# Turning x and the product with V in VectorE's blocks of 32 instead of on TensorE, in an attention kernel on one Trainium2 core

## The chip, the cores and the metric

The kernel runs on one core of a Trainium2 chip. Its time is the device time of one execution in microseconds (us). The median of three runs of the kernel before is 764.2 us (762.27 to 765.88). The profile is of one further execution, which took 762.58 us; the profile's span, from the first instruction of the program to the last, is 760.8 us of that.

Names: PE is TensorE, DVE is VectorE, ACT is ScalarE, POOL is GpSimd, SP is the engine whose queue issues most of the DMA transfers. PSUM is PE's output memory, eight banks of 128 x 512 f32.

## What is computed

x is 8 x 512 x 512 (batch, rows, model), cond is 8 x 512. There are 16 heads of 32 columns.

```
Q  = heads(x @ Wq.T + bq);     K  = heads(x @ Wk.T + bk);     V = heads(x @ Wv.T + bv)
tQ = heads(cond @ Wq.T + bq);  tK = heads(cond @ Wk.T + bk)      # one row per batch entry
scores = einsum('bhqd,bhkd->bhqk', Q + tQ, K + tK) / sqrt(32)
out = x + merge_heads(softmax(scores) @ V)
```

## The kernel before

The work is cut into T = 32 tiles: tile t is batch entry b = t // 4 and a group g = t % 4 of four heads (128 columns). PE, ACT, DVE and POOL run in the order that is written by hand (`manual_schedule`); SP's DMA queue runs in the order in which the program names the transfers.

**A tile.** Scores are made twice. `row_max` makes the scores of a chunk of 128 query rows (4 matmuls, one per head, into four banks), and DVE takes the negated maximum of each row (`row_max_of`, two reductions over two banks each). `denominators` has ACT take the exponential of the same banks with that maximum as bias; only the row sums (`sums`) are kept. `split_max` (POOL) splits the maximum into bf16 parts, and `transpose_max` turns them, so that `exponentials` can make the scores again in transposed form, keys by queries, with the maximum added by a matmul, and ACT writes their exponential to SBUF (`es`). `times_v` multiplies `es` by V: four heads go to four groups of 32 PSUM partitions, so the result is 128 (head, column) x 512 (query).

**The way out.** `weighted` does the four `times_v` of a tile and copies the result out of PSUM (`leave`, L556). Later `output` turns it back to query rows with four PE transposes (`untranspose`, L566), `divide` multiplies by the reciprocal of the sums (`invert`, L576; `divide`, L580), and `finish` (L591) adds x + bv on POOL and stores. x + bv is `xr`, loaded and summed by `load_residual` (L131, L135).

**The way in.** x comes in chunks of 128 rows (`load_x`, L123: 128 partitions, runs of 2 KB). `transpose_x` turns a chunk with four PE transposes (L251) and ACT or DVE copies it out of PSUM (L254) to `xT`. `combine_x` forms sums of quarters of `xT` for the projections, which multiply 2 x 2 blocks with seven products instead of eight (`first_products`, `other_products`, L335 and L338).

**The loop.** An iteration t has four stages, one for each key chunk of tile t; every stage has `exponentials(t, kc)`, a `row_max(t + 1, ...)`, the four `denominators` of it, and some other work between: stage 0 projects a part of the next batch entry's q and turns a chunk of x, stage 1 does `weighted(t - 1)`, stage 2 projects a part of k, stage 3 a part of v and `transpose_max`. `output(t - 1)` lies in stage 2 (t odd) or stage 3 (t even). Four iterations make one batch entry. The first tile and the weights are set up in an opening; the last three tiles have an order of their own after the loop.

**The banks.** `TURNS` lists, for eight consecutive stages (two iterations), which banks a stage uses: entries 0 to 3 for its exponentials (and then, as each comes free, for the stage's other work), entries 4 to 7 for the row scores. Pairs of entries that are read together are neighbouring banks before.

**The opening.** It loads x, cond and the weights, turns the weights (`transpose_w`, L206), projects tiles 0 and 1 in full (`project_qk`, L281) and makes the conditioning terms.

Of the kernel before, what the change touches and what calls it, by code (L numbers as in the profile page):

```python
# [17 lines left out]
def kernel(  # L18
# [32 lines left out]

    nc = tc.nc
# [25 lines left out]
    TURNS = [  # L78
        (7, 2, 0, 1, 3, 4, 5, 6),
        (7, 0, 3, 4, 5, 6, 1, 2),  # L80
        (3, 0, 4, 5, 1, 2, 6, 7),
        (2, 5, 0, 1, 6, 7, 3, 4),
        (7, 0, 5, 6, 3, 4, 1, 2),
        (3, 0, 4, 5, 1, 2, 6, 7),
        (4, 5, 0, 1, 6, 7, 2, 3),
        (5, 0, 6, 7, 1, 2, 3, 4),

        (2, 5, 6, 7, 3, 4, 0, 1),
        (2, 5, 3, 4, 0, 1, 6, 7),
        (2, 5, 0, 1, 6, 7, 3, 4),  # L90
        (2, 5, 6, 7, 3, 4, 0, 1),
        (2, 5, 3, 4, 6, 7, 0, 1),

        (2, 5, 0, 1, 6, 7, 3, 4),
        (2, 5, 3, 4, 6, 7, 0, 1),
        (0, 1, 5, 2, 6, 7, 3, 4),
        (0, 1, 5, 2, 6, 7, 3, 4),
        (5, 0, 6, 7, 1, 2, 3, 4),
# [3 lines left out]
    def banks(i, n=1):  # L102

        j = TURNS[turn[0]][i]
        return psum[:, j, :] if n == 1 else psum[:, j : j + n, :]
# [18 lines left out]

    xr = {}

    def load_residual(t):

        b, g = divmod(t, G)
        xr[t] = op.tile([P, NS, P], F32, tag="xr", name=f"xr_{t}", bufs=3)  # L130
        nc.sync.dma_start(  # L131
            xr[t], x[b].rearrange("(c p) d -> p c d", p=P)[:, :, g * P : (g + 1) * P]
        )
        bias = bvb[:, g * P : (g + 1) * P].unsqueeze(1).broadcast_to([P, NS, P])
        nc.gpsimd.tensor_tensor(xr[t], xr[t], bias, ALU.add)  # L135
# [28 lines left out]
    nc.sync.dma_start(cond_sb[:B, :], cond)  # L164
    nc.sync.dma_start(cond_sb[B : B + 1, :], bq.rearrange("(o d) -> o d", o=1))
    nc.sync.dma_start(cond_sb[B + 1 : B + 2, :], bk.rearrange("(o d) -> o d", o=1))
    load_w("q", Wq, nc.sync, [0])
    load_w("k", Wk, nc.scalar, [0])
    load_w("q", Wq, nc.scalar, [1])
    load_w("q", Wq, nc.sync, [2, 3])  # L170
# [3 lines left out]
    nc.sync.dma_start(bvb, bv.rearrange("(o d) -> o d", o=1).broadcast_to([P, D]))  # L174

# [8 lines left out]
    for i in range(2):  # L184
        m = const.tile([P, NS, HG, HD], BF16, tag=f"split{i}", name=f"split{i}")
        nc.vector.memset(m, 0.0)
        split.append(m)
    condT = const.tile([P, NC, HD], F32, tag="condT", name="condT")
# [54 lines left out]
    def transpose_x(n, pt, leaves=nc.vector.tensor_copy):  # L243

        b, sc = divmod(n, NS)
        if b >= B:
            return
        if sc == 0:
            xT[b] = xtp.tile([P, NC, S], F32, tag="xT", name=f"xT_{b}")
        for cc in range(NC):  # L250
            nc.tensor.transpose(  # L251
                pt[:, cc * P : (cc + 1) * P], xs[n][:, cc * P : (cc + 1) * P], ident
            )
        leaves(xT[b][:, :, sc * P : (sc + 1) * P], pt.rearrange("p (c s) -> p c s", c=NC))  # L254
        load_x(n + NS)
# [107 lines left out]
    def first_products(n, b, u, dens, small, at, first=0):  # L363

        one_, two_ = banks(first), banks(at)
        c1, c12, c2, c22 = parts_of(n, b, u)
        m1 = c2[:, 0, :]
        product(n, b, u, 1, one_[:, :HS])  # L370
        nc.scalar.copy(m1, one_[:, :HS])
        dens()
        small()
        product(n, b, u, 6, two_[:, :HS])
        w = P if n == "k" else HS
        product(n, b, u, 2, two_[:, HS : HS + w], (0,), slice(0, w))
        product(n, b, u, 7, one_[:, HS:])
        nc.vector.tensor_tensor(c12, two_[:, :HS], m1, ALU.add)
        nc.vector.tensor_tensor(c1[:, 0, :w], two_[:, HS : HS + w], m1[:, :w], ALU.add)
        if w < HS:  # L380
            nc.gpsimd.tensor_copy(c1[:, 0, w:], m1[:, w:])
        plus(n, b, u, 1, c22, one_[:, HS:], c12)
# [175 lines left out]
    def weighted(t, pt):  # L558

        for kc in range(NS):  # L560
            times_v(t, kc, pt)
        leave(t, pt)
# [68 lines left out]
    for c in range(NS):  # L631
        transpose_x(c, bank(1 + c), nc.scalar.copy if c % 2 else nc.vector.tensor_copy)
    pc = bank(6)
# [12 lines left out]
    transpose_w("q", 0, bank(7), 1)  # L646
    transpose_w("k", 0, bank(1), 0)
    transpose_w("q", 1, bank(2), 1)
    pq, pk = bank(5), bank(0)
    for cc in range(NC):  # L650
        project_qk_part(0, "q", cc, pq)
    transpose_w("q", 2, bank(3), 0)
    transpose_w("q", 3, bank(4), 1)
    for cc in range(NC):
        project_qk_part(0, "k", cc, pk)
    transpose_w("k", 1, bank(6), 0)
    condition("q", bank(7))
    transpose_w("k", 2, bank(1), 1)
    transpose_w("k", 3, bank(2), 0)
    transpose_w("v", 0, bank(3), 1)  # L660
    condition_end("q", bank(4), nc.vector)
    project_qk_end(0, "q", pq)
    condition("k", bank(6))
    transpose_w("v", 1, bank(7), 1)
    condition_end("k", bank(3), nc.gpsimd)
    transpose_w("v", 2, bank(1), 0)
    project_qk_end(0, "k", pk)
    transpose_w("v", 3, bank(4), 1)
    transpose_x(NS, bank(2), nc.scalar.copy)
# [9 lines left out]
    transpose_x(NS + 1, banks(0), nc.scalar.copy)  # L679
    denominators(0, 0)  # L680
    project_qk(1, "q", banks(3))
# [3 lines left out]
    transpose_x(NS + 2, banks(2), nc.scalar.copy)  # L685
# [8 lines left out]
    first_products("v", 0, 0, lambda: denominators(0, 3), nothing, 2, 0)  # L694
    advance()
    row_max(1, 0)
    transpose_max(0, banks(3), nc.scalar.copy)
    other_products("v", 0, 0, lambda: denominators(1, 0), nothing, (2, 0))
# [28 lines left out]
    for t in range(T - 3):  # L727
# [6 lines left out]
        if r % 2:  # L734
            turn_x = lambda: transpose_x(t + NS + 3, banks(1), nc.vector.tensor_copy)
            project_pair("q", *qk_of, dens, turn_x, 3)
        else:
            transpose_x(t + NS + 3, banks(0), nc.scalar.copy)
            if t:
                project_pair("q", *qk_of, dens, nothing, (1, 3))  # L740
            else:
                other_products("k", 0, 1, dens, nothing, (1, 3))
# [5 lines left out]
        if t:  # L748
            dens()
            invert(t - 1, sums[t - 1])  # L750
            weighted(t - 1, banks(0))
# [10 lines left out]
        if r % 2:  # L762
            project_pair("k", *qk_of, dens, lambda: output(t - 1, banks(1)), 3)
        elif t:
            project_pair("k", *qk_of, dens, nothing, (0, 2))
        else:
            other_products("v", 0, 1, dens, nothing, (0, 2))
# [5 lines left out]
        if t == T - 4:  # L773
            transpose_max(t + 1, banks(0), nc.scalar.copy)
            denominators(t + 2, 0)
            output(t - 1, banks(1))
# [4 lines left out]
        def small():  # L781
            transpose_max(t + 1, banks(1))
            if t and r % 2 == 0:
                output(t - 1, banks(2))

        project_pair("v", b + 1, r, dens, small, (0, 2) if r % 2 else 3)
# [47 lines left out]
    exponentials(t, 1, (3, 4, 6, 7))  # L834
# [4 lines left out]
    exponentials(t, 2, (3, 4, 0, 1))  # L839
    times_v(t, 1, pv)  # L840
    transpose_max(t + 1, pd)
    exponentials(t, 3, (6, 7, 3, 4))
    times_v(t, 2, pv)
    exponentials(t + 1, 0, (0, 1, 6, 7))
# [4 lines left out]
    exponentials(t, 1, (3, 4, 0, 1))  # L849
# [7 lines left out]
    exponentials(t, 2, (6, 7, 3, 4))  # L857
# [4 lines left out]
    exponentials(t, 3, (0, 1, 6, 7))  # L862
# [11 lines left out]
    pi, po = psum[:, 3, :], [psum[:, 4, :], psum[:, 6, :]]  # L874
# [55 lines left out]
```

## Time and profile before

| | |
|---|---|
| median of three runs | 764.2 us (762.27 to 765.88) |
| profiled execution: time, span | 762.58 us, 760.8 us |
| PE busy | 750.4 us, 99% of the span |
| ACT busy | 630.2 us, 83% |
| DVE busy | 525.2 us, 69% |
| POOL busy | 132.9 us, 17% |
| PE transposes of x: L251 | 128 in 32 groups of four |
| PE transposes of the product with V: L566 | 124 in 31 groups of four |
| DMA packets | 40376, of 29.51 MB |

Rows of the profile have the line in the kernel, the engine, the operation, output <- inputs and the shape; a group's busy time counts overlapped instructions once, and the end of a matmul is modelled. In the timeline the first two columns are the start and the length in us. "[0.67 <-PE psum L515]" at the end of a row means that the engine stood idle for 0.67 us before it, and that the instruction named ended that.

### The profile page before, as it was taken

The numbers are of one execution on the slowest core, as the hardware profiler recorded it, in microseconds if no ns is written. First come the engines' busy times: TensorE is split into PE (matmuls) and PEld (weight loads), VectorE is DVE, ScalarE is ACT, GpSimd is POOL, SyncE is SP. The second block draws the span as 40 slices with busy tenths as digits, with TensorE's granted clock in tenths as the row PEclk, the third lists the DMA queues.
The fourth block names the chain that finished last, engine by engine and source line by source line (L and its number), as shares of the span: only waits on it lengthen the run. The fifth ranks groups of instructions, "written<-read, shape, count | busy, mean of one in ns | idle before, by whom it ended". The sixth has DMA issues, their size and how long they took to land.

```text
span 760.8 us, 14393 instructions
## 1 busy us (share of the span) xinstructions
PE 750.4 (99%) x5494; PEld 435.9 (57%) x5494; DVE 525.2 (69%) x730; ACT 630.2 (83%) x1462; POOL 132.9 (17%) x229
## 2 busy tenths in 40 slices
PE   8999999999999999999999999999999999999997
PEld 5566556655556665565665555665555665555432
DVE  2577767677667777676776776777766777757764
ACT  2559888888889888888888888888888988888965
POOL 2711011111101111101111111111110111110220
PEclk9999999999999999999999999999999999999999
DMA  9200011102011110111111011110101111000110
GB/s 310 64 2 15 15 43 43 43 15 56 15 42 43 43 31 13 47 39 43 42 32 40 15 43 42 43 44 14 43 1 28 29 28 28 1 29 29 29 42 28
DMA packets 40376, 29.51 MB, mean 39 GB/s; under 512 B 1770, under 2 KB 34538, under 8 KB 40308
## 3 DMA queue, kind: packets, MB, share of 16 engines
q1 hardware_dynamic: 39460, 27.42, 12.6%
q10 hardware_dynamic: 848, 1.18, 0.5%
q8 instruction: 43, 0.70, 0.4%
q14 instruction: 25, 0.20, 0.1%
HBM read 20.21 MB, written 8.39 MB: 38 GB/s over the span
## 4 chain that ended last, share of the span: by engine, by line
PE 96%; ACT 1%; DMA 1%; DVE 0%; issue 0%; DVEq 0%
PE psum L338 25%; PE psum L534 15%; PE psum L515 15%; PE psum L433 14%; PE psum L335 14%; PE psum L512 6%; PE psum L566 2%; PE psum L251 2%; PE psum L281 2%; PE psum L496 1%; ACT e L527 1%; DMA w_k<-in_L_cond_Wk_dram 1%; PE psum L206 1%; ACT e L529 0%; DMA x<-in_x_dram 0%
## 5 line engine op out<-in xcount | busy, mean ns | idle before, releaser
L442 DVE TENSOR_REDUCE nmax<-psum 128x2 f32<-128x1024 f32 x256 | 301.7, 1219 | 160.1 <-PE psum L433 159.4
L470 ACT ACTIVATE dead<-psum,nmax 128x512 f32<-128x512 f32 x496 | 335.0, 692 | 12.9 <-DVE nmax L442 12.8
L527 ACT ACTIVATE e<-psum 128x512 f32<-128x512 f32 x270 | 145.8, 595 | 81.5 <-PE psum L515 81.5
L433 PE MATMUL psum<-kT,qT 32*128 32x512 f32 x1024 | 138.1, 595 | 0.7 <-ACT kT L296 0.4
L515 PE MATMUL psum<-qT,kT 32*128 32x512 f32 x1024 | 132.5, 588 | 0.0
L529 ACT ACTIVATE e<-psum 128x1024 f32<-128x1024 f32 x121 | 124.7, 1030 | 0.0
L534 PE MATMUL psum<-e,v 128*32 128x512 f32 x1024 | 118.6, 596 | 0.4 <-ACT e L529 0.3
L470 ACT ACTIVATION_READ_ACCUMULATOR dead<-psum,nmax 128x1 f32 x496 | 103.6, 209 | 0.0
L484 POOL CAST split<-nmax 128x16 bf16<-128x16 f32 x32 | 8.2, 255 | 510.8 <-DVE nmax L442 510.8
L433 PEld LDWEIGHTS psum<-kT,qT 32*128 32x128 f32 x1024 | 63.8, 183 | 51.8 <-issue 29.4
L534 PEld LDWEIGHTS psum<-e,v 128*32 128x32 f32 x1024 | 29.5, 109 | 82.1 <-issue 57.9
L512 PE MATMUL psum<-maxT,onesb 3*128 3x512 bf16 x512 | 51.4, 384 | 1.6 <-DVE res L580 0.8
L515 PEld LDWEIGHTS psum<-qT,kT 32*128 32x128 f32 x1024 | 51.1, 185 | 2.5 <-issue 0.2
L591 POOL TENSOR_TENSOR res<-res,xr 128x512 f32<-128x512 f32 x30 | 38.1, 1271 | 66.1 <-DVE res L580 66.1
L335 PE MATMUL psum<-wc_v,xc 128*128 128x256 f32 x192 | 49.4, 380 | 0.0
L512 PEld LDWEIGHTS <-onesb 3*128 3x128 bf16 x512 | 13.4, 91 | 60.5 <-issue 50.9
L338 PE MATMUL psum<-xc,wc_q 128*128 128x256 f32 x180 | 46.4, 380 | 0.3 <-ACT e L529 0.3
L338 PE MATMUL psum<-xc,wc_k 128*128 128x256 f32 x180 | 46.3, 379 | 0.0
L556 DVE COPY oT<-psum 128x512 f32<-128x512 f32 x29 | 20.1, 691 | 35.6 <-PE psum L534 35.6
L135 POOL TENSOR_TENSOR xr<-xr,bvb 128x512 f32<-128x512 f32 x32 | 40.6, 1270 | 0.0
L335 PE MATMUL psum<-wT_v,xT 128*128 128x256 f32 x128 | 37.9, 398 | 0.0
L335 PEld LDWEIGHTS psum<-wc_v,xc 128*128 128x128 f32 x192 | 35.4, 190 | 4.3
(147 smaller groups left out, 831.0 us busy)
## 6 DMA issues: line engine op xcount, KB each, us to landing
xr<-in_x_dram SPq DMA_DIRECT2D x32, 256.0 KB, 3.1
out_dram<-res SPq DMA_DIRECT2D x31, 256.0 KB, 2.4
x<-in_x_dram SPq DMA_DIRECT2D x30, 256.0 KB, 2.7
w_v<-in_L_cond_Wv_dram SPq DMA_DIRECT2D x4, 256.0 KB, 5.5
w_q<-in_L_cond_Wq_dram SPq DMA_DIRECT2D x3, 256.0 KB, 4.4
w_k<-in_L_cond_Wk_dram SPq DMA_DIRECT2D x3, 256.0 KB
x<-in_x_dram ACTq DMA_DIRECT2D x2, 256.0 KB, 4.1
w_k<-in_L_cond_Wk_dram ACTq DMA_DIRECT2D x1, 256.0 KB, 4.5
```

Source lines behind the costliest of these rows:

```text
L135: nc.gpsimd.tensor_tensor(xr[t], xr[t], bias, ALU.add)
L335: nc.tensor.matmul(pt, xb, w, start=(kc == kcs[0]), stop=(kc == kcs[-1]))
L338: nc.tensor.matmul(pt, w, xb, start=(kc == kcs[0]), stop=(kc == kcs[-1]))
L433: nc.tensor.matmul(pt, qkT["q", t][r, qc * P : (qc + 1) * P], qkT["k", t][r, :], start=True, stop=True,)
L442: nc.vector.tensor_reduce(nmax[t][:, qc, pr * 2 : pr * 2 + 2, 0], pt, AX.X, ALU.max, negate=True)
L470: nc.scalar.activation(dead, banks(HG + j), AF.Exp, bias=nmax[t][:, qc, j, :], accum_out=sums[t][:, qc, j, :],)
L512: nc.tensor.matmul(bank[j], onesb[r, :], maxT[t][r, :], start=True, stop=False)
L515: nc.tensor.matmul(bank[j], qkT["k", t][r, kc * P : (kc + 1) * P], qkT["q", t][r, :], start=False, stop=True,)
L527: nc.scalar.activation(e[:, i, :], bank[pr * 2 + i], AF.Exp)
L529: nc.scalar.activation(e, banks(2, 2), AF.Exp)
L534: nc.tensor.matmul(pt[j * HD : (j + 1) * HD, :], vs[b % 2][:, kc, (g * HG + j) * HD : (g * HG + j + 1) * HD], es[t, kc, j // 2][:, j % 2, ...
L591: last.tensor_tensor(y, y, xr.pop(t), ALU.add)
```

## The change

Four things change.

1. **x is loaded by blocks and turned by DVE** (from batch entry 1 on). `spread` views a 512 x 512 matrix so that partition j of a group of 32 holds the rows j, 32 + j, 64 + j and so on, 32 columns of each: a run of 128 bytes per row. `load_block` loads the 128 columns of a chunk so, with four DMAs of 32 partitions. One DVE transpose of 32 x 32 blocks (`turn_x`) then gives a chunk of `xT` in SBUF; neither PE nor PSUM is used. The chunks are now columns, not rows.
2. **The product with V is turned by DVE** for the tiles 0 to 27 (`weighted`). The transpose reads PSUM and writes `y` with queries modulo 32 on partitions. The sums have to take the same arrangement: POOL spreads them (`apart`, 128 x 64), and four small matmuls (128 x 32 weights `modulo`, 16 columns, one per head), placed after the first `times_v`, bring them to a bank `pd`; DVE takes the reciprocal from there. POOL then multiplies, adds `xr` (now loaded by blocks too) and four DMAs store runs of 128 bytes. `leave`, `untranspose`, `divide` and `output` fall away for these tiles; tiles 28 to 31 keep the old way.
3. **TURNS** is another table, since the turns of x and of the product need no bank of their own; pairs may lie apart, and are read with a step. The entries used by the projections change with it.
4. **The opening** issues cond, bq and bk from ACT's queue, the first chunk of Wk and the second of Wq from SP's, adds constants (`which`, `modulo`, `bvs`), and projects q of tile 1 at the place where a chunk of x was turned.

```diff
+    def spread(a, d):
+        return a.rearrange("(f j) d -> j f d", j=BL)[:, :, d : d + BL]
+
+    def load_block(n):
+        b, cc = divmod(n, NC)
+        if b < B:
+            xs[n] = xp.tile([P, NB, BL], F32, tag="x", name=f"x_{n}")
+            for h in range(HG):
+                nc.sync.dma_start(xs[n][h * BL : (h + 1) * BL], spread(x[b], cc * P + h * BL))
...
+    def turned_by_vector(t):
+        return t < T - 4
...
+        if turned_by_vector(t):
+            xr[t] = op.tile([P, NB, BL], F32, tag="xr", name=f"xr_{t}", bufs=3)
+            for h in range(HG):
+                nc.sync.dma_start(
+                    xr[t][h * BL : (h + 1) * BL], spread(x[b], g * P + h * BL)
+                )
...
-    nc.sync.dma_start(cond_sb[:B, :], cond)
-    nc.sync.dma_start(cond_sb[B : B + 1, :], bq.rearrange("(o d) -> o d", o=1))
-    nc.sync.dma_start(cond_sb[B + 1 : B + 2, :], bk.rearrange("(o d) -> o d", o=1))
+    nc.scalar.dma_start(cond_sb[:B, :], cond)
+    nc.scalar.dma_start(cond_sb[B : B + 1, :], bq.rearrange("(o d) -> o d", o=1))
+    nc.scalar.dma_start(cond_sb[B + 1 : B + 2, :], bk.rearrange("(o d) -> o d", o=1))
     load_w("q", Wq, nc.sync, [0])
-    load_w("k", Wk, nc.scalar, [0])
-    load_w("q", Wq, nc.scalar, [1])
-    load_w("q", Wq, nc.sync, [2, 3])
+    load_w("k", Wk, nc.sync, [0])
+    load_w("q", Wq, nc.sync, [1, 2, 3])
...
-        load_x(n + NS)
+        load_block(n + NC)
+
+    def turn_x(n):
+        b, cc = divmod(n, NC)
+        if b >= B:
+            return
+        if cc == 0:
+            xT[b] = xtp.tile([P, NC, S], F32, tag="xT", name=f"xT_{b}")
+        nc.vector.transpose(xT[b][:, cc, :], xs[n].rearrange("p f i -> p (f i)"))
+        load_block(n + NC)
...
-    def weighted(t, pt):
+    def weighted(t, pt, pd):
+        apart = op.tile([P, HG, NS, NS], F32, tag="apart", name=f"apart_{t}")
+        nc.gpsimd.tensor_tensor(
+            apart,
+            sums[t].rearrange("p c h o -> p h c o").broadcast_to([P, HG, NS, NS]),
+            which.unsqueeze(1).unsqueeze(1).broadcast_to([P, HG, NS, NS]),
+            ALU.mult,
+        )
         for kc in range(NS):
             times_v(t, kc, pt)
-        leave(t, pt)
+            if kc == 0:
+                for h in range(HG):
+                    nc.tensor.matmul(
+                        pd[h * BL : (h + 1) * BL, : NB],
+                        modulo,
+                        apart[:, h].rearrange("p c a -> p (c a)"),
+                        start=True,
+                        stop=True,
+                    )
+        rec = op.tile([P, NB, 1], F32, tag="recs", name=f"recs_{t}")
+        nc.vector.reciprocal(rec, pd[:, :NB].unsqueeze(2))
+        y = op.tile([P, NB, BL], F32, tag="res", name=f"res_{t}")
+        nc.vector.transpose(y.rearrange("p f e -> p (f e)"), pt)
+        nc.gpsimd.tensor_tensor(y, y, rec.broadcast_to([P, NB, BL]), ALU.mult)
+        nc.gpsimd.tensor_tensor(y, y, xr.pop(t), ALU.add)
+        b, g = divmod(t, G)
+        for h in range(HG):
+            nc.sync.dma_start(spread(out[b], g * P + h * BL), y[h * BL : (h + 1) * BL])
...
-            invert(t - 1, sums[t - 1])
-            weighted(t - 1, banks(0))
+            weighted(t - 1, banks(0), banks(1))
...
-            project_pair("k", *qk_of, dens, lambda: output(t - 1, banks(1)), 3)
-        elif t:
-            project_pair("k", *qk_of, dens, nothing, (0, 2))
-        else:
-            other_products("v", 0, 1, dens, nothing, (0, 2))
+        if t:
+            project_pair("k", *qk_of, dens, nothing, 1 if r % 2 else (0, 3))
+        else:
+            other_products("v", 0, 1, dens, nothing, (0, 3))
```

The rows of TURNS that the prediction speaks of, for the stages 1 and 2 of an even and of an odd iteration:

```diff
-        (7, 0, 3, 4, 5, 6, 1, 2),
-        (3, 0, 4, 5, 1, 2, 6, 7),
+        (7, 2, 0, 1, 3, 4, 5, 6),
+        (3, 0, 1, 2, 6, 7, 4, 5),
...
-        (3, 0, 4, 5, 1, 2, 6, 7),
-        (4, 5, 0, 1, 6, 7, 2, 3),
+        (6, 7, 0, 1, 4, 5, 2, 3),
+        (4, 7, 0, 1, 2, 3, 5, 6),
```

## The prediction, made before the change was run

> **What bounds the kernel now.** I read the busy table first, then the busy time by stretches of one batch entry, then the timeline of two iterations, then the groups and the DMA queues.
>
> ```profile
> span 760.8 us, 14393 instructions
> ...
> PE 750.4 (99%) x5494; PEld 435.9 (57%) x5494; DVE 525.2 (69%) x730; ACT 630.2 (83%) x1462; POOL 132.9 (17%) x229
> ```
>
> ```profile
> core 0: us, PE busy (x) PEld busy (x) DVE busy (x) ACT busy (x) POOL busy (x), PEclk, DMA share, GB/s
> 175.00:265.00 90.00, 90.00 (x676) 53.23 (x672) 64.78 (x90) 78.87 (x184) 14.25 (x26) 1.00 0.13 36
> ```
>
> One stretch of 90 us is nearly one batch entry (four tiles; it repeats every 90.4 us in the timeline). PE has no gap in it; ACT has 11.1 us, DVE 25.2 us, and the granted clock is 1.00. So time goes where PE's time goes, but only what PE really issues less counts, and busy time overstates that, since ends of matmuls are modelled and overlap. The timeline gives the true price, from one start to the next:
>
> ```profile
> 306.80 0.60 PE L251 MATMUL psum<-ident,x 128*128 128x128 f32 x4
> 307.24 1.03 PE L338 MATMUL psum<-xc,wc_q 128*128 128x256 f32 x4
> ...
> 315.11 0.39 PE L512 MATMUL psum<-maxT,onesb 3*128 3x512 bf16 x4
> 315.31 0.69 DVE L556 COPY oT<-psum 128x512 f32<-128x512 f32 x1 [1.12 <-PE psum L534]
> ...
> 316.20 1.02 PE L433 MATMUL psum<-kT,qT 32*128 32x512 f32 x8
> 316.39 1.08 ACT L527 ACTIVATE e<-psum 128x512 f32<-128x512 f32 x2 [0.67 <-PE psum L515]
> ...
> 321.88 1.09 ACT L527 ACTIVATE e<-psum 128x512 f32<-128x512 f32 x2 [0.45 <-PE psum L515]
> ...
> 346.26 0.66 PE L566 MATMUL psum<-ident,oT 128*128 128x128 f32 x4
> 346.75 1.03 PE L335 MATMUL psum<-wc_v,xc 128*128 128x256 f32 x4
> ```
>
> Four transposes of x hold PE for 307.24 - 306.80 = 0.44 us, four of the output for 346.75 - 346.26 = 0.49 us (in the other iteration the two change places). The last field of the ACT rows is ACT's spare time ahead of a stage: 0.67 and 0.45 us.
>
> ```profile
> L251 PE MATMUL psum<-ident,x 128*128 128x128 f32 x128 | 20.1, 285 | 0.1
> L556 DVE COPY oT<-psum 128x512 f32<-128x512 f32 x29 | 20.1, 691 | 35.6 <-PE psum L534 35.6
> L566 PE MATMUL psum<-ident,oT 128*128 128x128 f32 x124 | 19.6, 280 | 0.0
> L580 DVE TENSOR_TENSOR res<-psum,rec 128x512 f32<-128x512 f32 x31 | 21.1, 681 | 1.4 <-PE psum L566 1.0 <-POOL split L484 0.4
> ```
>
> **PE.** 28 of the 32 groups of x transposes go (batch entry 0 keeps its four) and 28 of the 31 output groups. By busy time that is 112 x 157 ns + 112 x 158 ns = 35.3 us; by starts it is 56 x 0.47 = 26.3 us, and I use that. Added are four small matmuls per tile. An f32 matmul counts twice in the trace (32 instructions for the 16 of `times_v`), so eight instructions. The row nearest in form is L534, the same 128 x 32 weights in four column groups: its sets of four start together, so the eight are two sets. Their 16 columns hide no weight load, so I charge two exposed loads of 109 ns (L534's PEld row) and a little streaming: 0.25 us. Low end: hidden but for streaming, 0.06 us. High end: the four 10-column transposes of the opening (L636, from 6.74 to the next matmul at 7.08) take 0.34 us, twice that is 0.68 us. Over 28 tiles: 7 us, between 2 and 19. Net on PE: -26.3 + 7.0 = -19.3 us.
>
> **The new wait on PE.** The small matmuls wait for `apart`; behind them stand three `times_v` and all later stages. `apart` needs sums that were complete an iteration earlier, and about 0.25 us of POOL (the 16-column POOL rows take 230 to 269 ns). POOL could be late only if it stands at the add of `xr`, waiting for its load. That load is issued in the previous iteration's stage 2 or 3, at the latest after the four stores, some 8 us ahead, and lands 3.1 us after issue now. I cost it at nothing; without this cover each late us is a PE us.
>
> **DVE.** Per tile it loses the copy 0.691, the divide 0.681 and the reciprocal 0.243, and the four-per-entry copies of x, of which it did two (0.682) and ACT two (0.60). It gains a transpose of the product, one of x, and a reciprocal from PSUM. A transpose is not in the trace. The nearest row is L556, the same 128 x 512 out of PSUM, 0.69 us. The Trainium skill, VectorE: DVE Perf Modes, section on the three transpose paths, gives 311 ns for 128 x 128 bf16 and blocks of 32 x 32 only; four times that is an estimate of 1.24 us. At 0.69 DVE per batch entry goes from 64.8 to 64.8 - 7.8 + 6.5 = 63.5 us: no bound. The place that matters is the bank. The product's bank (entry 0 of TURNS in stage 1: 7 or 6) is a score bank of the next stage (entries 6, 7, 4, 5 and 2, 3, 5, 6), as it is before. The old copy starts at 315.31, the scores at 316.20: 0.89 us, into which 0.69 fits. At 1.24 PE would wait about 0.4 us per tile, 28 x 0.4 = 11 us; a DVE faster than the copy gains nothing there, since PE doesn't wait now. The sum uses 0.69 for both transposes, the row; by the rule it would be 11 us less gain. Behind the transpose on DVE stand `combine_x` and the next reductions; the old copy stood in the same place.
>
> **ACT** loses the copies of x, 1.2 us per entry: 78.9 - 1.2 = 77.7 in a new period of 90.4 - 8 x 0.47 + 4 x 0.25 = 87.6 us, 89%. The tightest stage is stage 2 of an odd iteration, where 0.45 us was spare and 0.44 goes. So ACT is just not late; I charge 0 to 4 us over the run, 1 in the sum.
>
> **POOL** gains a multiply (1.27, as L591) and `apart`: 14.3 + 4 x 1.5 = 20.3 us per entry. Its two operations on the product end about 3.6 us after the stage starts; `split_max`, queued behind, waits for a maximum that comes later (POOL was idle 15 us before it). Nothing.
>
> **DMA and SP's queue.** Per tile a block of x, `xr` and the store are 3 x 2048 packets of 128 B in twelve DMAs, instead of 1152 packets in three.
>
> ```profile
> q1 hardware_dynamic: 39460, 27.42, 12.6%
> ...
> 349.80:353.00 3.20, 3.20 (x27) 2.00 (x20) 1.81 (x2) 2.71 (x5) 0.00 (x0) 1.00 0.60 166
> ```
>
> The stretch holds a store and an `xr` load in packets of 512 B: 0.60 x 16 x 3.2 us = 30.7 us of engine time for 166 GB/s x 3.2 us = 531 KB, 30 ns a packet. A packet of 128 B costs between a quarter of that and the whole; I take the whole. Then 384 packets per engine and tile are 11.5 us of the 21.9 us that a tile lasts. Here the Trainium skill speaks against the change: DMA: Bandwidth & Descriptors, Specifications, says that transfers below 512 B miss line rate because the engine reads, modifies and writes. If a store so costs double, it is 128 x 60 + 256 x 30 = 15.4 us, still under 21.9. The queue becomes the bound only from 21.9 / 384 = 57 ns for every packet. By rule and row the sum is the same, nothing. SP issues an `xr` DMA of 512 runs in 0.50 us, so twelve take 6 us of 21.9. SP's waits: block loads stand behind the DVE transpose, stores behind POOL's add, and `xr` loads behind the stores; x has four tiles of lead, `xr` two thirds of one. The stores have two buffers.
>
> **The opening.** PE waits there for Wk's first chunk:
>
> ```profile
> 8.89 0.63 PE L206 MATMUL psum<-ident,w_k 128*128 128x128 f32 x4 [1.16 <-DMA w_k<-in_L_cond_Wk_dram]
> ```
>
> ACT issued it at 4.22, having waited for x. From SP it goes earlier: up to -1.2 us. Against that cond now leaves on ACT's queue as late, and is wanted at 6.73; nine small DVE constants come before x lands at 4.2 (DVE is idle from 1.9); 20 more DMAs follow the weights. I take -1.2, between -2 and +3. The tail keeps its order.
>
> **The sum.** -26.3 + 7.0 + 1.0 - 1.2 = -19.5 us. The profiled execution took 762.58 us (span 760.8 and 1.8 around it): 743.1. It lies 1.6 below the median of 764.2, so the same change puts the median at 744.7; executions spread by 3.6 us, and I say 744.
>
> **The rivals.**
> *The gain is half lost to a new wait* (0.15). The DVE transpose takes 1.24 us, or the small matmuls 0.68: -19.5 + 11 = -8.5 or -19.5 + 12 = -7.5, so 755 to 757. For it: one margin is 0.2 us, the other was not measured. Against it: the rows nearest in form.
> *Slower: the DMA engines become the bound* (0.16). Every load and store of the loop is 128 B; from 57 ns a packet the queue falls behind, then `xr` comes late, POOL stands, and `apart` holds PE. At 70 ns a tile lasts 384 x 0.070 = 26.9 us: 28 x (26.9 - 21.9) = 140 us more than 744, so 884; just above the point, at 64 ns, 24.6 us and 820; at 60 ns 776. For it: the skill's rule, and no 128 B packet in the trace to look at. Against it: 512 B take 30 ns.
> *The turns leave PE but ACT sets the period* (0.05): the spare 0.45 us are used up and exponentials come late everywhere, within 0.5% of 764 (760 to 768). Against it: 89% and stages of uneven length that level out.
> *All as summed* (0.64): 734 (free small matmuls, a good opening) to 752.
>
> **How the numbers follow.** A difference of 0.5%, 3.8 us, is about what the measurement tells from none. Faster: 0.64 + 0.15 = 0.79. Same 0.05. Slower 0.16. The range 734 to 762 takes in the first case and the half-lost one, and leaves out the slow case and a few hundredths beyond 734.
>
> **What would show it.** Right: L251 with 16 matmuls, L566 with the few of the opening and the last tiles, a transpose row on DVE near 0.69 us, PE still without gaps at a period near 87.6 us, DMA share below 0.6. Wrong: a PE wait named after DVE's transpose or POOL's `apart`; a DVE transpose over 0.9 us; DMA share near 1 with landings of `xr` over 8 us; ACT without idle time before L527; L433 waiting for ACT.

## The result, and the profile after

The changed kernel takes 751.78 us (median of four runs, 751.59 to 752.0). The kernel before, run beside it, takes 763.98 us (762.27 to 765.88). The ratio is 0.9838, with a 95% interval of 0.982 to 0.9857. That is a gain of 12.2 us where some 20 were forecast: the sign and the range held, the size did not. The profiled execution took 751.59 us, its span is 749.8 us.

The page of the kernel after, busy table, queue and two groups:

```profile
span 749.8 us, 14920 instructions
...
PE 736.8 (98%) x5494; PEld 411.7 (55%) x5494; DVE 529.4 (71%) x727; ACT 621.6 (83%) x1446; POOL 178.6 (24%) x285
...
q1 hardware_dynamic: 184112, 28.01, 21.7%
...
L639 DVE STREAM_TRANSPOSE res<-psum 128x512 f32<-128x512 f32 x28 | 20.1, 717 | 34.4 <-PE psum L591 18.0
...
L641 POOL TENSOR_TENSOR res<-res,xr 128x512 f32<-128x512 f32 x28 | 39.9, 1425 | 2.2
```

PE lost 13.6 us of busy time and the span 11.0 us. The transpose of the product takes 0.717 us. POOL's add takes 1.425 us on average, although it is the operation that took 1.271 us before (L591): something slows it. The same stretch of one batch entry, by the busy time of each engine:

```profile
core 0: us, PE busy (x) PEld busy (x) DVE busy (x) ACT busy (x) POOL busy (x), PEclk, DMA share, GB/s
175.00:265.00 90.00, 89.64 (x684) 50.25 (x680) 65.20 (x89) 78.67 (x185) 20.87 (x34) 1.00 0.23 36
```

PE now has 0.36 us without work in it. ACT works as long as before, although its two copies of x per entry are gone, because 90 us now hold more than one batch entry. The useful view is the length of each stage: from one L512 row (L569 after) to the next in the timeline. Two iterations, which are two tiles, have eight stages:

| us | even: stage 0 | 1 | 2 | 3 | odd: 0 | 1 | 2 | 3 | two tiles |
|---|---|---|---|---|---|---|---|---|---|
| before, every pair | 5.66 | 5.62 | 5.50 | 6.08 | 5.70 | 5.62 | 5.50 | 5.54 | 45.22 |
| after, r = 2 and 3 | 5.26 | 5.77 | 5.50 | 5.63 | 5.27 | 5.75 | 5.06 | 5.85 | 44.09 |
| after, r = 0 and 1 | 5.26 | 5.77 | 5.50 | 6.01 | 5.27 | 5.75 | 5.06 | 6.46 | 45.08 |

The four stages that lost a set of transposes became shorter by 0.40, 0.45, 0.43 and 0.44 us (1.72 together). Stage 1, which got the small matmuls, grew by 0.14 us. So far this is near the forecast (0.47 us a set, 0.25 us). Two things are not. Stage 3 of the odd iteration grew by 0.31 us although nothing was added to it. And in the first two iterations of each batch entry (r = 0 and 1, the ones with `combine_x`) stage 3 is longer by another 0.38 and 0.61 us. A batch entry takes 44.09 + 45.08 = 89.2 us, against 90.4 before and 87.6 in the forecast. The first stage starts at 53.78 us instead of 55.45, so the opening gave 1.7 us.

**Where the 0.31 us come from.** The timeline of the kernel after, stages 2 and 3 of an odd iteration (r = 3):

```profile
309.52 0.39 PE L569 MATMUL psum<-maxT,onesb 3*128 3x512 bf16 x4
309.65 0.72 DVE L639 STREAM_TRANSPOSE res<-psum 128x512 f32<-128x512 f32 x1 [1.20 <-PE psum L591]
...
310.80 1.08 ACT L584 ACTIVATE e<-psum 128x512 f32<-128x512 f32 x2 [0.77 <-PE psum L572]
...
314.58 0.39 PE L569 MATMUL psum<-maxT,onesb 3*128 3x512 bf16 x4
...
314.80 1.03 PE L572 MATMUL psum<-qT,kT 32*128 32x512 f32 x8
...
315.02 0.69 ACT L527 ACTIVATE dead<-psum,nmax 128x512 f32<-128x512 f32 x1
...
315.86 1.08 ACT L584 ACTIVATE e<-psum 128x512 f32<-128x512 f32 x2
315.86 0.31 PEld L490 LDWEIGHTS psum<-kT,qT 32*128 32x128 f32 x8 [0.86 <-ACT dead L527]
315.86 1.14 PE L490 MATMUL psum<-kT,qT 32*128 32x512 f32 x8
...
320.43 0.40 PE L569 MATMUL psum<-maxT,onesb 3*128 3x512 bf16 x4
```

PE's stage 2 is 314.58 - 309.52 = 5.06 us long. ACT's exponentials start at 310.80 and at 315.86: 5.06 us apart, with no idle field on the second row. ACT is busy through the whole stage. Its last exponential for the row sums (315.02) still reads the bank that the next stage's scores want, so their weight load waits 0.86 us for it, and PE's next stage is 320.43 - 314.58 = 5.85 us long. The table of waits says the same for the whole run. First the kernel before, then the kernel after (us in total, times, longest):

```profile
ACT dead L470 <- DVE nmax L442: 12.8, 63, 1.5
PEld psum L433 <- ACT dead L470: 12.2, 51, 0.4
```

```profile
ACT dead L527 <- DVE nmax L499: 35.1, 84, 5.1
PEld psum L490 <- ACT dead L527: 33.2, 71, 0.9
```

The second line of each pair is the weights of PE's scores waiting for ACT: from 12.2 to 33.2 us. Such a wait is not time lost one for one, since PE still multiplies during most of it (here to 315.83): the 0.86 us at this place, 14 times, are 12.0 of the 33.2, and cost 0.31 us each. The first line is ACT waiting for DVE's maximum: from 12.8 to 35.1 us. Of that rise 8.8 us belong to the other loss (it is 26.3 in e1, where that loss is gone).

**Where the 0.99 us per batch entry come from.** The rows of four lines of the kernel after, with shortest, median and longest duration in ns, behind the rows of the first two in the kernel before (L265 and L268 there):

```profile
L265 DVE TENSOR_TENSOR xc<-xc,xT x7: 691/691/694, 67.8 to 610.3; 128x512 f32<-128x512 f32 x7
```

```profile
L268 DVE TENSOR_TENSOR xc<-xT,xc x7: 685/685/687, 90.4 to 633.0; 128x512 f32<-128x512 f32 x7
```

```profile
L322 DVE TENSOR_TENSOR xc<-xc,xT x7: 691/1423/1424, 65.7 to 600.5; 128x512 f32<-128x512 f32 x7
```

```profile
L325 DVE TENSOR_TENSOR xc<-xT,xc x7: 1534/1537/1537, 87.8 to 622.8; 128x512 f32<-128x512 f32 x7
```

```profile
L640 POOL TENSOR_TENSOR res<-res,recs x28: 1046/1047/1404, 87.4 to 689.1; 128x512 f32<-128x512 f32 x28
```

```profile
L641 POOL TENSOR_TENSOR res<-res,xr x28: 1267/1278/1607, 88.9 to 690.2; 128x512 f32<-128x512 f32 x28
```

L322 and L325 are the second operations of `combine_x`; they took 0.69 us before. Only where they run beside POOL's two new operations on y do both engines slow down: the one short L322 is that of iteration 0, in which no product is turned. One such place (even iteration, r = 0) in the timeline:

```profile
331.66 0.72 DVE L639 STREAM_TRANSPOSE res<-psum 128x512 f32<-128x512 f32 x1 [1.26 <-issue]
...
332.30 0.65 DVE L321 TENSOR_TENSOR xc<-xT 128x512 f32<-128x512 f32 x1
332.46 1.40 POOL L640 TENSOR_TENSOR res<-res,recs 128x512 f32<-128x512 f32 x1 [15.44 <-DVE res L639]
...
332.98 1.42 DVE L322 TENSOR_TENSOR xc<-xc,xT 128x512 f32<-128x512 f32 x1
...
333.94 1.60 POOL L641 TENSOR_TENSOR res<-res,xr 128x512 f32<-128x512 f32 x1
...
334.33 2.34 DVE L499 TENSOR_REDUCE nmax<-psum 128x2 f32<-128x1024 f32 x2
...
335.57 0.69 ACT L527 ACTIVATE dead<-psum,nmax 128x512 f32<-128x512 f32 x1 [0.82 <-DVE nmax L499]
```

The Trainium skill has the rule for it: SBUF — State Buffer, section "Who interferes with whom", says that a VectorE instruction with two SBUF inputs contends with a GpSimd instruction that reads SBUF, that what they share is locked for one of them at a time, and that the order of issue decides which one is blocked. The trace agrees, nearly. POOL's L640 is issued at 332.46 while L321, which reads two parts of `xT`, runs until 332.95; with its usual 1.05 us it would end at 334.00, and ends at 333.86. DVE's L322 is issued at 332.98; behind L640 and with its usual 0.69 us it would end at 334.55, and ends at 334.40. L641 behind L322 would end at 335.67, and ends at 335.54. So they take turns, each instruction for itself, and 0.13 to 0.15 us of each overlap. The result is that the reductions, queued behind `combine_x` on DVE, start about 0.7 us late, ACT's exponentials are late with them (0.82 us idle at 335.57; 0.16 at the same place in e1), and the next stage's scores are late because of ACT.

### The profile page after: what moved, and what is told of

Same layout as the page of the kernel before. It is cut to its first block, busy times and chain, and to the rows that moved or that the text cites. A ratio compares the mean times of both kernels' runs of the same rounds, so it can differ in the third digit from the quotient of the medians.

```text
span 749.8 us, 14920 instructions
## 1 busy us (share of the span) xinstructions
PE 736.8 (98%) x5494; PEld 411.7 (55%) x5494; DVE 529.4 (71%) x727; ACT 621.6 (83%) x1446; POOL 178.6 (24%) x285
## 3 DMA queue, kind: packets, MB, share of 16 engines
q1 hardware_dynamic: 184112, 28.01, 21.7%
## 4 chain that ended last, share of the span: by engine, by line
PE 84%; DVE 7%; ACT 5%; issue 2%; DMA 1%; ACTq 0%; DVEq 0%
PE psum L395 20%; PE psum L591 15%; PE psum L490 14%; PE psum L392 14%; PE psum L572 12%; PE psum L569 5%; ACT dead L527 4%; DVE nmax L499 2%; PE psum L338 2%; DVE xc L325 1%; DVE res L639 1%; DVE xc L322 1%; PE psum L553 1%; PE psum L254 1%; DVE xc L324 1%
## 5 line engine op out<-in xcount | busy, mean ns | idle before, releaser
L527 ACT ACTIVATE dead<-psum,nmax 128x512 f32<-128x512 f32 x496 | 334.1, 686 | 35.3 <-DVE nmax L499 35.1
L490 PE MATMUL psum<-kT,qT 32*128 32x512 f32 x1024 | 141.0, 605 | 1.6 <-ACT e L586 0.3
L640 POOL TENSOR_TENSOR res<-res,recs 128x512 f32<-128x512 f32 x28 | 33.9, 1212 | 435.3 <-DVE res L639 435.3
L572 PE MATMUL psum<-qT,kT 32*128 32x512 f32 x1024 | 134.6, 589 | 0.0
L591 PE MATMUL psum<-e,v 128*32 128x512 f32 x1024 | 120.3, 596 | 1.0 <-ACT e L586 0.8
L527 ACT ACTIVATION_READ_ACCUMULATOR dead<-psum,nmax 128x1 f32 x496 | 101.4, 204 | 0.0
L490 PEld LDWEIGHTS psum<-kT,qT 32*128 32x128 f32 x1024 | 58.8, 183 | 64.5 <-ACT dead L527 33.2
L591 PEld LDWEIGHTS psum<-e,v 128*32 128x32 f32 x1024 | 26.9, 110 | 65.8 <-issue 41.1
L569 PE MATMUL psum<-maxT,onesb 3*128 3x512 bf16 x512 | 54.6, 384 | 2.8 <-ACT dead L527 1.2
L569 PEld LDWEIGHTS <-onesb 3*128 3x128 bf16 x512 | 14.4, 91 | 63.8 <-issue 54.2
L639 DVE STREAM_TRANSPOSE res<-psum 128x512 f32<-128x512 f32 x28 | 20.1, 717 | 34.4 <-PE psum L591 18.0
L641 POOL TENSOR_TENSOR res<-res,xr 128x512 f32<-128x512 f32 x28 | 39.9, 1425 | 2.2
L395 PEld LDWEIGHTS psum<-xc,wc_q 128*128 128x128 f32 x180 | 34.2, 190 | 4.6
```

Source lines behind the costliest of these rows:

```text
L395: nc.tensor.matmul(pt, w, xb, start=(kc == kcs[0]), stop=(kc == kcs[-1]))
L490: nc.tensor.matmul(pt, qkT["q", t][r, qc * P : (qc + 1) * P], qkT["k", t][r, :], start=True, stop=True,)
L527: nc.scalar.activation(dead, banks(HG + j), AF.Exp, bias=nmax[t][:, qc, j, :], accum_out=sums[t][:, qc, j, :],)
L569: nc.tensor.matmul(bank[j], onesb[r, :], maxT[t][r, :], start=True, stop=False)
L572: nc.tensor.matmul(bank[j], qkT["k", t][r, kc * P : (kc + 1) * P], qkT["q", t][r, :], start=False, stop=True,)
L591: nc.tensor.matmul(pt[j * HD : (j + 1) * HD, :], vs[b % 2][:, kc, (g * HG + j) * HD : (g * HG + j + 1) * HD], es[t, kc, j // 2][:, j % 2, ...
```

## The experiments

All times stand against the kernel before in the same runs. Unless said otherwise, an edit is made to the kernel after. The changed kernel's own ratio, 0.9838, is what the variants of it compare with.

**e1: `combine_x` ahead of the transpose.** Its operations go between the reciprocal and the transpose of the product in `weighted`, so that they are over when POOL begins.

```diff
-    def weighted(t, pt, pd):
+    def weighted(t, pt, pd, between):
...
         nc.vector.reciprocal(rec, pd[:, :NB].unsqueeze(2))
+        between()
         y = op.tile([P, NB, BL], F32, tag="res", name=f"res_{t}")
...
-            weighted(t - 1, banks(0), banks(1))
+            weighted(
+                t - 1, banks(0), banks(1), lambda: combine_x(b + 1, r) if r < 2 else None
+            )
         else:
             first_products("v", 0, 1, dens, nothing, 1)
-        if r < 2:
             combine_x(b + 1, r)
```

> The changed kernel, with the two DVE operations of combine_x put between the reciprocal and the transpose of the product, ahead of POOL's two operations on y instead of beside them. Theory A (DVE operations with two SBUF inputs and POOL operations beside them slow each other): the second operation of combine_x falls from 1.42 and 1.54 us to 0.69, POOL's multiply and add from 1.40 and 1.60 to 1.05 and 1.27, the stages of 6.01 and 6.46 us go back to 5.63 and 5.85, and the time to about 746 (7 batch entries x 0.99 us less, about 1 us given back because the transpose of the product starts 0.2 us later). Theory B (DVE is late because it now has the transposes to do, or because packets of 128 B disturb SBUF): the second operation stays long, and the time stays within 1 us of 751.8.

745.25 us (745.21 to 745.73), ratio 0.9756 (0.9738 to 0.9773). Every pair of tiles from the second to the fourteenth now takes 44.08 to 44.10 us; the longer stages are gone. The second operation of `combine_x`, both of its lines, and POOL's add in this kernel:

```profile
L322 DVE TENSOR_TENSOR xc<-xc,xT x7: 691/692/693, 66.4 to 593.6; 128x512 f32<-128x512 f32 x7
```

```profile
L325 DVE TENSOR_TENSOR xc<-xT,xc x7: 678/678/679, 86.5 to 615.6; 128x512 f32<-128x512 f32 x7
```

```profile
L642 POOL TENSOR_TENSOR res<-res,xr x28: 1267/1274/1279, 89.2 to 684.4; 128x512 f32<-128x512 f32 x28
```

All have their usual durations again, on both engines. This version beats both kernels, and lies 1 us above the 744 that was forecast for the change.

**e2: POOL's work on y left out** in the iterations with `combine_x`; the order on DVE stays.

```diff
-        nc.gpsimd.tensor_tensor(y, y, rec.broadcast_to([P, NB, BL]), ALU.mult)
-        nc.gpsimd.tensor_tensor(y, y, xr.pop(t), ALU.add)
+        if (t + 1) % G >= 2:
+            nc.gpsimd.tensor_tensor(y, y, rec.broadcast_to([P, NB, BL]), ALU.mult)
+            nc.gpsimd.tensor_tensor(y, y, xr.pop(t), ALU.add)
```

> The changed kernel, without POOL's multiply and add on y for those tiles whose product is turned in an iteration with combine_x (half of them; their output is stored undivided and without x). DVE's order, the transposes and the transfers stay. Theory A: both operations of combine_x take 0.65 to 0.69 us, stage lengths as without combine_x (5.63 and 5.85), about 745. Theory B: the second operation of combine_x stays at 1.42 and 1.54 us and the time within 1 us of 751.8.

746.19 us (745.43 to 747.06), ratio 0.9767 (0.9748 to 0.9786); L322 takes 0.691 us and L325 0.680, and the same pairs take 44.07 to 44.10 us. In e1 the place in DVE's order had changed, here it has not: what the two have in common is that DVE and POOL don't overlap there.

**e5: long runs.** The same bytes and the same tiles, but x, the residual and the output move in runs of 2 KB and 512 B, in one DMA each. The diff shows x; the other two are changed in the same way.

```diff
-            for h in range(HG):
-                nc.sync.dma_start(xs[n][h * BL : (h + 1) * BL], spread(x[b], cc * P + h * BL))
+            nc.sync.dma_start(
+                xs[n].rearrange("p f i -> p (f i)"), x[b, cc * P : (cc + 1) * P, :]
+            )
```

> The changed kernel, with the same bytes moved in the old runs: blocks of x and xr as 128 rows of 2 KB, the store in runs of 512 B, one DMA each instead of four (rows and columns are not in the places that the computation wants, so the output is not the reference's). Theory (the packets of 128 B cost nothing, the queue has a share of 0.23): within 1 us of 751.8. Rival (they disturb DVE or POOL in SBUF, or delay xr): 746 or less, with the second operation of combine_x below 1.4 us.

752.37 us (752.33 to 753.65), ratio 0.9845 (0.9822 to 0.9869): no gain. The stages are those of the kernel after to 0.01 us in both kinds of pairs (44.09 and 45.08), but for two stages of the profiled execution (one in the tail), 1.8 us together; so the contention isn't one with the DMA. The queue did become lighter:

```profile
q1 hardware_dynamic: 29552, 27.99, 12.9%
```

**e3: ACT's copy for k on DVE.** ACT's 0.37 us copy of the first product of k goes to DVE, to free ACT in stage 2.

```diff
-        nc.scalar.copy(m1, one_[:, :HS])
+        if n == "k":
+            nc.vector.tensor_copy(m1, one_[:, :HS])
+        else:
+            nc.scalar.copy(m1, one_[:, :HS])
```

> The changed kernel, with the copy of k's first product (0.37 us on ACT in stage 2 of the odd iterations) moved to DVE. Theory (ACT sets the length of that stage and delays the scores of the next, which wait for its last exponential): stage 3 of an odd iteration falls from 5.85 by 0.2 to 0.3 us, 14 times, so about 748 to 749. Rival (DVE's last addition for k, which also frees banks for the next scores, is as late as ACT): it then ends 0.4 us later, and the time stays at 751 to 753.

760.9 us (760.55 to 762.34), ratio 0.9964 (0.9954 to 0.9974): much slower than the kernel after. In the iterations without `combine_x`, stage 3 of the odd iteration did fall from 5.85 to 5.54 us, as the theory of ACT has it. But stage 2 grew from 5.06 to 5.99:

```profile
317.30 0.41 DVE L429 COPY kT<-psum 128x256 f32<-128x256 f32 x1
...
317.77 1.13 PE L395 MATMUL psum<-xc,wc_k 128*128 128x256 f32 x4 [0.67 <-DVE kT L429]
```

DVE comes to the copy only after its two reductions, and PE's later products go to the bank from which it is taken. PE waits 0.67 us for it. The edit moved the work onto a queue that is taken just then, so as a test of ACT it is spoilt: a second thing changed.

**e4: the edits of e1 and e3 together** (the two diffs above).

> The moves of combine_x and of k's copy together. If both causes hold and are separate, the savings add: about 743, near the 743 to 744 that the sum for the change had given. If only the first holds, 746.

754.3 us (754.21 to 754.46), ratio 0.9873 (0.9856 to 0.989). The pairs take 44.70 us (one 44.99). Against e1 that is 9.1 us more, as e3 is against the kernel after: the two losses add up, with no part in common.

**e11: one exponential less.** With the edit of e1; in odd iterations one of the four exponentials for the row sums of stage 2 is left out on ACT, and POOL writes a constant in place of its sums.

```diff
+        if last < HG:
+            nc.gpsimd.memset(sums[t][:, qc, last:, :], 256.0)
-        for j in [pr * 2 + i for pr in prs for i in range(2)]:
+        for j in [pr * 2 + i for pr in prs for i in range(2)][:last]:
...
-        dens = lambda: denominators(t + 1, 3)
+        dens = lambda: denominators(t + 1, 3, last=HG - 1 if r % 2 else HG)
```

> The changed kernel with combine_x ahead of the weighted step's transposes (as in e1, 745.25 us), and one of the four exponentials for the row sums of stage 2 of every odd iteration left out on ScalarE (its row sums are set to a constant instead, so those rows are scaled wrongly). Theory (ScalarE has become the bound of that stage: 5.06 us of work in a stage of 5.06 us, and the next stage's scores wait for its last such exponential): with 0.69 us of its work gone, stage 3 of the odd iteration falls from 5.85 us to the 5.54 us of the kernel before, 14 x 0.31 = 4.3 us, time about 741 us. Rival (the bank comes free as late anyway, by VectorE's last work on it, or the products are what is late there): stage 3 stays at 5.85 us and the time at 745 us.

741.26 us (740.97 to 742.65), ratio 0.9713 (0.9688 to 0.9738). Stage 3 of the odd iteration takes 5.54 us, all other stages are as in e1, and a pair takes 43.77 us. The next stage's exponentials and scores in the timeline:

```profile
311.33 0.19 PEld L490 LDWEIGHTS psum<-kT,qT 32*128 32x128 f32 x4 [0.24 <-DVE kT L418]
...
311.76 1.02 PE L490 MATMUL psum<-kT,qT 32*128 32x512 f32 x8
...
311.95 1.08 ACT L586 ACTIVATE e<-psum 128x512 f32<-128x512 f32 x2 [0.72 <-PE psum L574]
```

The scores begin 1.09 us into the stage (it starts at 310.67) instead of 1.28 us (314.58 to 315.86 above), and run in 1.02 us instead of 1.14. Their weights are loaded from 0.66 us on, after 0.24 us of waiting for DVE, where they waited 0.86 for ACT, which now has 0.72 us to spare. Stage 2 itself stays at 5.06 us: PE sets its length, and ACT's work in it sets when the next scores begin. The late ACT costs 14 x 0.31 = 4.3 us; the medians of e1 and e11 differ by 4.0.

**e6: the queues of the opening undone:** cond, bq and bk go back to SP's queue, the first chunk of Wk and the second of Wq to ACT's.

```diff
-    load_w("k", Wk, nc.sync, [0])
-    load_w("q", Wq, nc.sync, [1, 2, 3])
+    load_w("k", Wk, nc.scalar, [0])
+    load_w("q", Wq, nc.scalar, [1])
+    load_w("q", Wq, nc.sync, [2, 3])
```

> The changed kernel, with the loads of the opening on their old queues (cond, bq and bk from SP, the first chunk of Wk and the second of Wq from ACT). If the queues gave the opening's gain, the loop starts 1.2 to 1.7 us later and the time is 753 to 753.5; if the work taken from PE there gave it, nothing changes.

752.91 us (752.32 to 753.84), ratio 0.9849 (0.9826 to 0.9873). The stages stay the same, and the first one starts at 55.39 us, as before the change (55.45); the kernels with the new queues and the same opening start it at 53.8 to 54.5 us. So the queues seem to give the gain of the opening, near 1 us, but that rests on one execution of each. The times don't settle it: the medians differ by 1.1 us, but the intervals of the two ratios overlap, and e5, with the new queues, has nearly the ratio of e6.

**e7: x alone turned by DVE,** on the kernel before, with its table and its entries.

```diff
-            turn_x = lambda: transpose_x(t + NS + 3, banks(1), nc.vector.tensor_copy)
-            project_pair("q", *qk_of, dens, turn_x, 3)
+            project_pair("q", *qk_of, dens, nothing, 3)
...
-            transpose_x(t + NS + 3, banks(0), nc.scalar.copy)
...
+        turn_x(t + NS + 3)
```

> The kernel before with x alone loaded by blocks and turned by DVE; the product keeps its PE transposes, banks and opening queues as before. By PE's starts 28 groups of 0.47 us leave: 13 us, so 751, if nothing else waits. POOL has no new work, so combine_x stays at 0.69 us. If ACT's chain takes a part back, 754 to 757.

763.24 us (761.88 to 765.72), ratio 0.9991 (0.9971 to 1.001). PE issues four transposes less per tile, and the stages are what they were: 5.64, 5.62, 5.50, 6.09, 5.69, 5.62, 5.50, 5.54. The projection in stage 0 of an odd iteration shows why:

```profile
308.32 1.13 PE L362 MATMUL psum<-xT,wT_q 128*128 128x256 f32 x4
...
309.61 0.73 PEld L362 LDWEIGHTS psum<-xc,wc_q 128*128 128x128 f32 x4 [0.56 <-ACT e L553]
309.61 1.13 PE L362 MATMUL psum<-xc,wc_q 128*128 128x256 f32 x4 [0.16 <-ACT e L553]
```

The second group of products starts 1.29 us after the first, and waits for ACT's second exponential, a pair of banks, to free its bank (entry 3). In the kernel after it is 0.97 us, because there the entry is 1 and the bank comes free with the first exponentials:

```profile
300.55 1.13 PE L395 MATMUL psum<-xT,wT_q 128*128 128x256 f32 x4
...
301.52 1.03 PE L395 MATMUL psum<-xc,wc_q 128*128 128x256 f32 x4
```

In the kernel before the transposes lay in this wait.

**e8: the product alone turned by DVE,** on the kernel before: `weighted` of the kernel after, `output` dropped, the old table and entries.

```diff
-            project_pair("k", *qk_of, dens, lambda: output(t - 1, banks(1)), 3)
+            project_pair("k", *qk_of, dens, nothing, 3)
...
-            if t and r % 2 == 0:
-                output(t - 1, banks(2))
```

> The kernel before with the product alone turned by DVE; x keeps its PE transposes. By PE's starts 28 groups of 0.47 us leave, 28 x 0.14 come for the sums: 9 us less. Theory A takes 7 x 0.99 us of it back in combine_x: about 762, nearly nothing gained. Without theory A: 755.

765.65 us (764.42 to 767.8), ratio 1.0024 (1.0009 to 1.0038). Stage 3 of the even iteration falls from 6.08 to 5.69 us; stage 2 of the odd one stays at 5.49, and has the same wait:

```profile
319.77 1.13 PE L370 MATMUL psum<-xc,wc_k 128*128 128x256 f32 x4 [0.16 <-ACT e L561]
```

Stage 1 grows to 5.68, and in the pairs with `combine_x` the contention comes back (45.74 us instead of 44.94). Together they eat the gain.

**e9: e7 with half of the new entries:** the new TURNS table, pairs read with a step, and the new entries of stage 0 (1 and (0, 3)); stage 2 keeps its old ones.

```diff
-            project_pair("q", *qk_of, dens, nothing, 3)
+            project_pair("q", *qk_of, dens, nothing, 1)
...
-                project_pair("q", *qk_of, dens, nothing, (1, 3))
+                project_pair("q", *qk_of, dens, nothing, (0, 3))
```

> The kernel with x alone turned by DVE, which gained nothing, now with the first eight rows of the changed TURNS, their reader with a step, and the changed entries for the projection in stage 0 (second bank 1, or 0 and 3); stages 1 to 3 keep the entries and the PE transposes of the output. Theory C (the x transposes filled a wait of PE for the projection's second bank, which the pair of exponentials frees; without them PE waits as long, until the bank is changed): stage 0 falls from 5.69 and 5.64 to about 5.26, 14 x 0.8 us, so about 752 if the other stages keep their lengths. Theory D (stage 0 is as long for another reason, ACT or DVE): it stays at 5.6 to 5.7 and the time at 763.

772.0 us (770.18 to 773.06), ratio 1.0097 (1.007 to 1.0124). Stage 0 falls to 5.26 and 5.36 us, near the 5.26 and 5.27 of the kernel after, so the wait of e7 goes with the entry. But stage 3 of the even iteration grows to 6.93 us: DVE's last step of k in stage 2 (L388) reads a bank (entry 2, bank 1) that is the fourth of the next stage's exponentials on the new table.

```profile
347.04 0.37 PE L539 MATMUL psum<-maxT,onesb 3*128 3x512 bf16 x1 [0.57 <-DVE kT L388]
```

**e10: the kernel after with the old entries** on the new table.

```diff
-            project_pair("q", *qk_of, dens, nothing, 1 if r % 2 else (0, 3))
+            project_pair("q", *qk_of, dens, nothing, 3 if r % 2 else (1, 3))
...
-            project_pair("k", *qk_of, dens, nothing, 1 if r % 2 else (0, 3))
+            project_pair("k", *qk_of, dens, nothing, 3 if r % 2 else (0, 2))
```

> The changed kernel, with the entries of the kernel before for the projections of q and k (3 and (1, 3) in stage 0, 3 and (0, 2) in stage 2) on the changed TURNS. Theory C: PE waits for the pair of exponentials again, stages 0 go from 5.26 to about 5.65, stage 2 of odd iterations from 5.06 to about 5.5; up to 14 x 1.2 us, so 760 to 768. Theory D: stages 0 stay at 5.26 and the time within 2 us of 751.8.

777.43 us (777.29 to 778.09), ratio 1.0173 (1.0148 to 1.0199): the same PE transposes are gone as in the kernel after, and it is slower than before the change. The stages 0 take 5.64 and 5.69 us, as in e7, and stage 3 of the even iteration 6.49 or 6.86. Both waits are there, that for ACT's second exponential and that for DVE's last addition to k:

```profile
301.94 0.37 PE L569 MATMUL psum<-maxT,onesb 3*128 3x512 bf16 x1 [0.57 <-DVE kT L418]
...
322.61 1.13 PE L395 MATMUL psum<-xc,wc_k 128*128 128x256 f32 x4 [0.16 <-ACT e L586]
```

## Why the prediction was right, and where it was short

The direction and the range came out, and 751.78 us lies at the upper end of the case "all as summed" (734 to 752). Of the gain that was summed little more than half was measured. Term by term, over the run:

| term of the sum | predicted | measured |
|---|---|---|
| 56 sets of PE transposes gone | -26.3 (0.47 us each) | -24.1 (1.72 us for four, 0.43 each) |
| small matmuls, 28 tiles | +7.0 (0.25) | +3.9 (0.14) |
| ACT in stage 2, odd iterations | +1.0 | 14 x 0.31 = +4.3 |
| DVE beside POOL | 0 | 6 x 0.99 + 0.61 = +6.6 |
| opening | -1.2 | -1.7 in the profiled execution |
| sum | -19.5 | -11.0; the spans differ by 11.0 |

The first batch entry of the loop has only the longer of its two stages, 0.61 us, since iteration 0 turns no product.

**The price of PE by starts** was nearly right: 24.1 us against 26.3, where busy time would have given 35.3. With both mis-sized terms taken away (e11), a batch entry takes 2 x 43.77 = 87.5 us, against the 87.6 that the step worked out. That it is so near is luck: the transposes were priced 0.3 us per entry too high, the small matmuls 0.4 us, and the two errors cancel.

**DVE's transpose** was taken at the 0.69 us of the copy that it replaces, and not at the 1.24 us worked out from the Trainium skill (VectorE: DVE Perf Modes, the three transpose paths). It takes 0.717 us out of PSUM and 0.70 out of SBUF. The product's bank is free in time, and no matmul of PE waits for the transpose or for `apart`. The first rival, half of the gain lost to one of these two prices, gives a time (755 to 757) not far from the measured one, but by mechanisms that did not occur.

**The DMA engines** never came near to being the bound. The queue's 21.7% of 16 engines over 749.8 us is 2603 us of engine time, by 184112 packets, nearly all of them of 128 bytes, 14.1 ns each, where 30 were taken as the high end. The stretch shows a share of 0.23. The rule of the Trainium skill (DMA: Bandwidth & Descriptors, Specifications) on transfers under 512 bytes speaks for a loss; in e5 no cost of it shows.

**The step that failed most** is the POOL paragraph with its "Nothing", and "no bound" for DVE. I asked whether each engine had time, and whether what stands behind it in its own queue would wait. I did not ask whether the two could run side by side. `combine_x` stood right behind the old copy too, so the order on DVE looked unchanged; new was that the same event, the end of the transpose, releases POOL's work on y at that moment. e1 and e2 show it from both sides: the same stages with DVE's part moved and with POOL's part gone.

**The other one** is ACT: "0 to 4 us, 1 in the sum". The place was named, with its spare 0.45 us against 0.44 that go, and the mechanism was the one named. It cost 4.3 us. The error was to read the spare time as if a stage that fits to 0.01 us were still free: ACT's last exponential then ends later than the next scores begin to want its bank. Two of the prediction's own signs of being wrong are there: the scores wait for ACT (0.86 us), and ACT has no idle time before its exponentials (315.86). The rival "ACT sets the period" is true of one stage in eight.

**What the prediction took as given** was that a transpose that PE does not issue is time gained. By e7 and e8 it is so only if the table and the entries change along with it: on the old ones PE waits for ACT in the same place, and the parts alone give nothing (0.9991) or lose (1.0024). By e10 the full change with the old entries on the new table loses 1.7%; no run has the full change on the old table. The term of PE came out because the change has them; the working did not say that it rests on them.

**The opening** gave 1.7 us in the profiled execution, where 1.2 was taken; the medians of e6 give 1.1, within their noise. The wait for Wk's first chunk is gone, but PE now waits for cond: 0.52 us in this execution, 1.32 in that of e1.

It stays open why the small matmuls cost 0.14 us; no run took them out alone.

## What to carry to other kernels

When work moves to DVE and POOL, look not only at how full each queue is but at what runs at the same instant: two SBUF inputs on DVE beside a POOL instruction took turns, and moving 1.3 us of DVE work ahead of the event that releases POOL gave back 6.5 us of 752. Work taken off the bounding engine is worth what the next wait in that place leaves of it, so look up who frees the bank that the next instruction writes; buffers and order are part of the saving. A stage that another engine just fills has no margin: price it as a loss of the next stage.

## What the hardware showed that was not expected

- Here DVE instructions with two SBUF inputs and POOL's element-wise ones took turns (128 x 512 f32): 0.69 us became 1.42 and 1.54 us on DVE, and 1.05 became 1.40 and 1.27 became 1.60 us on POOL, with an overlap of only 0.13 to 0.15 us.
- A DVE transpose of 128 x 512 f32 in blocks of 32 x 32 takes 0.70 to 0.72 us, about what a copy of that shape takes (0.69).
- Packets of which nearly all have 128 bytes cost 14.1 ns of a DMA engine in the mean, loads and stores together; twelve DMAs of such runs per tile raised the share in the loop from 0.13 to 0.23, and long runs in their place (e5) gained no time.
- Eight f32 matmul instructions of 16 columns in four column groups lengthened a stage of `times_v` by 0.14 us, though by starts PE goes on to the next row 0.06 us later.
